# Pair preparation, scatters and shared expert taken out of the fixed order and emitted behind the scan

## The chip, the cores and the metric

The kernel runs on one core of one Trainium2 chip. The core has TensorE (PE, with its weight loads shown apart as PEld), VectorE (DVE), ScalarE (ACT), GpSimd (POOL) and SyncE (SP), each with a queue of its own that is worked off in order. The metric is the device time of one execution in microseconds; lower is better. Before the change the median of 13 runs is 1127.09 us (1125.89 to 1131.21).

## The reference

One layer of an adaptively modulated transformer block on `x` of shape (8, 512, 128), in float32:

```python
mod = (silu(c) @ wmod).reshape(8, 6, 1, -1)
sa, ca, ga, sb, cb, gb = ...           # the six parts; |ga|, |gb| at least 0.25
h = layernorm(x) * (1 + ca) + sa
x = x + ga * mamba(h)                  # 4 layers, then an RMS norm with final_norm_w
h = layernorm(x) * (1 + cb) + sb
x = x + gb * moe(h)
```

A layer of `mamba` norms `h`, projects it, runs a causal convolution of four taps with SiLU, a state-space scan over the 512 positions (8 heads of 32, state 128), a gated RMS norm and an output projection that is added to `h`. `moe` norms its input again, sends every token through a shared expert (128 to 512, ReLU, 512 to 128) and through the two experts of eight with the largest router probabilities, weighted by these, and adds the results:

```python
normed = h * rsqrt(mean(h * h) + 1e-8) * norm_weight
shared = relu(normed @ sw1 + sb1) @ sw2 + sb2
scores, idx = top_k(sigmoid(normed @ router_w.T), 2)
w = scores / (scores.sum(-1) + 1e-6)
routed = sum over the two: w * (relu(normed @ ew1[e] + eb1[e]) @ ew2[e] + eb2[e])
```

## The kernel before

**The scan.** A unit is one of the 8 sequences in one of the 4 layers (32 units), an item is a chunk of 128 positions of a unit (`NI` = 128 items). A loop over `t` emits the stages of several items, shifted against each other: the projections and the convolution of a unit run 16 steps (`LEAD * NC`) ahead of its items. From `p >= NI`, that is for the last 16 items, there is no next unit to project. For an item, `decay_rows` (L819) loads the cumulative decay row broadcast over the partitions, `decay_diff` (L838) subtracts on POOL, `decay_mask` masks on POOL, `decay_exp` (L859) takes the exponential on ACT, `mix` (L905) multiplies on DVE, `chunk_out` and `state_out` are products on TensorE, `state_decay` (L935, POOL) and `state_next` (L947) carry the state, `gate` (L984) and `project_out` (L994) follow, and `out_add` (L1018) adds the result to the residual `hs`, scaled by an inverse root that POOL takes (L1015). For the last 13 items `whole` (L834) is 4 instead of 8: POOL subtracts for four heads only, and ACT takes the other four as exponentials with the bias `ncum`, the negated sum that L809 writes.

**Pairs.** When two sequences have left the last layer, `rejoin` (L332) prepares them for the experts. It loads the modulation (`md`, L341), takes the final RMS norm (squares on ACT, `mean_squares` L320; inverse root by POOL for the first two pairs and by `power` L306 with small DVE instructions for the others; scaling on ACT, L356; product with `md` on DVE, L360), adds to `x`, takes the layer norm with its modulation, the second RMS norm, transposes the rows (L407), multiplies with the router weights (L415), chooses two experts for each token (L440 to L459), counts how many tokens of earlier columns and pairs go to each expert (`taken`, one table after the other), and puts 16 scatters per pair on a list: each writes 128 rows of the normed input with weight and token number to the list of their experts in DRAM, by `scatter` (L498) on POOL.

**Shared expert.** `shared` (L537) takes one sequence at a time: four products into four PSUM banks (L575), a ReLU out of each on ACT (L542), 16 products into one bank (L553) and a copy to `accs` (L546). It may run up to two evacuations late (`evacuate`). The hidden values take one of the five buffers that the scan's `xbc` has too.

**What sets the order.** The scan loop lies in `tc.manual_schedule()`: every engine issues its instructions in the order in which they are emitted. `rejoin`, `shared` and `tables` are generators, and the loop advances them at fixed places of a step: `rejoin` (`step_pairs`) once between `state_next` and `gate`, and once at the end of the step; `shared` (`serve`) once at the end of the step; one scatter per step ahead of `mix`. A pair begins two steps after its last item. What is left when the loop ends is woven by a second region of fixed order (from L1317), in which only POOL's order is left to the scheduler; it also holds `tables` (L1211, which expert each of the 39 tiles of 256 rows belongs to), `fetch` (L1256, loads of an expert's weights and, as `rest`, of its rows) and the loop over the tiles with `turn`, `hidden` and `combine`. Outside a fixed region the scheduler decides, from its own estimates of when operands are ready, where an instruction stands among the others of its engine; instructions emitted earlier have the higher priority.

**Buffers.** During the scan, pairs and the shared expert take PSUM banks from `pbank` (three banks). Behind it, pairs take them from three more (`psD`), and row buffers from a second pool (`frow2`, two buffers of each kind, as `frow`); `held` makes a pair wait where its row buffers are still to be scattered.

## Time and profile before

| | us |
|---|---|
| median of 13 runs | 1127.09 |
| profiled execution | 1127.32 |
| its span | 1124.9 |
| PE busy | 960.9 (85%) |
| DVE busy | 828.4 (74%) |
| ACT busy | 768.1 (68%) |
| POOL busy | 828.7 (74%) |
| last `out_add` of the scan ends | 840.6 |
| first scatter of the last pair starts | 909.5 |
| first `turn` on TensorE starts | 937.5 |

Times in the profile count from the start of the span. The busy shares are means over stages with different limits, so they don't tell what a change in one stage is worth. The profiled execution is one run; the 2.4 us between its span and its time lie around the span. A group "L862 ACT dV<-dV" is the instruction of line 862 on ACT that reads and writes the tile `dV`; the time after an arrow is how long the engine stood idle before, and what ended it. "remote" is a wait whose release the profile doesn't show. Float32 products show as two records each.

### The profile page before, as it was taken

To read this page: it belongs to the slowest core of one execution; us is meant where nothing else is said; L and a number is where in the kernel's file an instruction comes from. 1 tells how busy PE (TensorE), PEld (TensorE's weight loads), DVE (VectorE), ACT (ScalarE), POOL (GpSimd) and SP (SyncE) were. 2 spreads that over 40 slices of the span, in tenths; PEclk is the share of its full clock that TensorE was granted. 3 is DMA by queue.
4 is the path that set the end of the run, shared out by engine and by line. 5 is a ranking of instruction groups with operands and counts; after the bars stand their busy time and mean duration, and the time that the engine had idled before them with its cause. 6 is when DMAs were issued, how large, how long until landed. Compare 5 with 4: busy or idle time off the path is not lost. (4 is left out here: it accounts for less than half of the span.)

```text
span 1124.9 us, 21442 instructions
## 1 busy us (share of the span) xinstructions
PE 960.9 (85%) x7130; PEld 731.7 (65%) x7130; DVE 828.4 (74%) x1990; ACT 768.1 (68%) x1725; POOL 828.7 (74%) x841
## 2 busy tenths in 40 slices
PE   3667899999999999999999998687758756999985
PEld 1335677777777677777767776565545545888882
DVE  3758889889989889989889998586546163666653
ACT  4577998988988889889889878786336322333320
POOL 6868888989989989889989888685651552555550
PEclk9668999999999999999999999787867887999998
DMA  5141444655655555643424343422000125777756
GB/s 113 5 143 59 137 153 128 186 160 169 195 168 170 187 154 175 171 150 123 129 97 135 113 131 126 135 98 85 29 29 10 38 72 153 220 220 216 224 141 228
DMA packets 134301, 151.18 MB, mean 134 GB/s; under 512 B 22568, under 2 KB 106696, under 8 KB 134192
## 3 DMA queue, kind: packets, MB, share of 16 engines
q1 hardware_dynamic: 127184, 137.91, 41.4%
q0 software_dynamic: 4672, 9.42, 2.5%
q10 hardware_dynamic: 2336, 2.50, 0.7%
q8 instruction: 56, 0.92, 0.3%
q14 instruction: 53, 0.43, 0.1%
HBM read 120.07 MB, written 29.71 MB: 133 GB/s over the span
## 5 line engine op out<-in xcount | busy, mean ns | idle before, releaser
L698 DVE SCALAR_TENSOR_TENSOR xbc<-px,cw,xbc 128x511 f32<-128x511 f32 (+2 forms) x384 | 285.8, 745 | 31.4 <-ACT xbc L688 24.3
L841 POOL TENSOR_TENSOR dV<-dV,cum 128x1024 f32<-128x1024 f32 (+1 forms) x128 | 231.7, 1810 | 0.0
L907 DVE TENSOR_TENSOR dV<-dV,ptx 128x1024 f32<-128x1024 f32 x128 | 155.1, 1212 | 16.1 <-ACT xT L885 15.4
L849 POOL TENSOR_SCALAR_AFFINE_SELECT dV<-dV 128x1024 f32<-128x1024 f32 x128 | 141.7, 1107 | 9.3
L892 POOL TENSOR_TENSOR xd<-xT,dt 128x512 f32<-128x512 f32 (+1 forms) x128 | 120.5, 941 | 34.6 <-ACT xT L885 34.6
L500 POOL DMA_INDIRECT yg<-y,ix x78 | 84.1, 1078 | 83.9 <-DVE y L1313 69.4
L862 ACT ACTIVATE dV<-dV 128x1024 f32<-128x1024 f32 (+1 forms) x128 | 129.1, 1009 | 13.1 <-POOL dV L849 12.7
L500 POOL DMA_INDIRECT xg<-row,ix x64 | 63.4, 990 | 63.4 <-ACT hds L542 42.1
L688 ACT ACTIVATE xbc<-px,cbias,cw 128x512 f32<-128x512 f32 x128 | 99.3, 776 | 10.1 <-PE px L677 9.7
L677 PE MATMUL px<-hT,Wi 128*128 128x512 f32 x192 | 100.4, 605 | 0.0
L916 PEld LDWEIGHTS py<-xbc,st 128*128 128x128 f32 x384 | 61.3, 203 | 55.3 <-issue 38.0
L991 ACT ACTIVATE sq<-g 128x256 f32<-128x256 f32 x128 | 52.4, 410 | 58.3 <-DVE g L987 39.3
L1295 ACT ACTIVATE hd<-ph,bs 128x256 f32<-128x256 f32 x78 | 32.7, 470 | 83.4 <-PE ph L1289 74.4
L1007 PE MATMUL po<-Wo,g 128*128 128x128 f32 x512 | 89.4, 298 | 0.0
L1003 PEld LDWEIGHTS po<-ones,sq 128*128 128x128 f32 x512 | 68.3, 194 | 31.2 <-issue 21.3
L975 PE MATMUL py<-dV,xd 128*32 128x128 f32 x2048 | 85.4, 286 | 0.0
L965 PEld LDWEIGHTS py<-xbc,dg 128*128 128x128 f32 x512 | 79.0, 201 | 6.8 <-issue 1.0
L1003 PE MATMUL po<-ones,sq 128*128 128x1 f32 x512 | 78.7, 258 | 5.0 <-ACT sq L991 4.6
L965 PE MATMUL py<-xbc,dg 128*128 128x128 f32 x512 | 81.5, 284 | 0.0
L1302 PE MATMUL pe<-w,hd 128*128 128x128 f32 x624 | 75.9, 275 | 0.0
L1289 PE MATMUL ph<-xt,w 128*128 128x256 f32 x312 | 74.9, 384 | 0.1
L1302 PEld LDWEIGHTS pe<-w,hd 128*128 128x128 f32 x624 | 72.7, 192 | 0.1
(249 smaller groups left out, 2269.8 us busy)
## 6 DMA issues: line engine op xcount, KB each, us to landing
dV<-crow SPq DMA_DIRECT2D x128, 512.0 KB
w<-in_L_ffn_ew_dram SPq DMA_DIRECT2D x78, 256.0 KB
xg<-blank SPq DMA_DIRECT2D x64, 260.0 KB
ecum<-crow SPq DMA_DIRECT2D x256, 48.0 KB
rows<-xg SPq DMA_DIRECT2D x39, 130.0 KB
b<-in_L_ffn_eb_dram SPq DMA_DIRECT2D x39, 64.0 KB
x<-in_L_attn_x_dram SPq DMA_DIRECT2D x8, 256.0 KB
md<-mods SPq DMA_DIRECT2D x8, 256.0 KB
```

Of the source, the lines that this page charges most:

```text
L500: i = nc.gpsimd.indirect_dma_start(out=to, out_offset=bass.IndirectOffsetOnAxis(ap=ix, axis=0), in_=of, in_offset=None)
L677: nc.tensor.matmul(px[v, k][:, :L], Wi[l][:, c0 : c0 + P], hT[v], start=True, stop=True)
L688: nc.scalar.activation(xbc[v][:, k, :], px[v, k][:, :L], AF.Identity, bias=cbias[:, l, k : k + 1], scale=cw[:, l, k, KT - 1 : KT],)
L698: nc.vector.scalar_tensor_tensor(xbc[v][:, k, d:], px[v, k][:, : L - d], cw[:, l, k, KT - 1 - d : KT - d], xbc[v][:, k, d:], ALU.mult, ALU ...
L841: nc.gpsimd.tensor_tensor(dV[i][:, :w], dV[i][:, :w], cums[g][:, h0 : h0 + w].unsqueeze(2).to_broadcast([P, w, Q]), ALU.subtract,)
L849: nc.gpsimd.affine_select(out=dV[i], in_=dV[i], pattern=[[0, NH], [1, Q]], compare_op=ALU.is_ge, fill=-1e30, base=0, channel_multiplier=-1,)
L862: nc.scalar.activation(dV[i][:, :w], dV[i][:, :w], AF.Exp)
L892: nc.gpsimd.tensor_mul(xds[i][:, :w], xv.unsqueeze(1).to_broadcast([P, w, NH, HD]), dts[g][:, :w, h0 : h0 + NH].unsqueeze(3).to_broadcast( ...
L907: nc.vector.tensor_mul(Ms[i], Ms[i], pg.pop(i).unsqueeze(1).to_broadcast([P, NH, Q]))
L965: nc.tensor.matmul(py[i][:, k, :], dg[l][:, k, :], xbc[u][:, k, t], start=False, stop=True, skip_group_check=True,)
L1003: nc.tensor.matmul(pp[:, 2 * DM + c : 2 * DM + c + 1], sq[:, k, :], ones[:, 0:1], start=(k == 0), stop=(k == NB - 1))
L1302: nc.tensor.matmul(pe[:, s, :], hd[:, k, s * P : (s + 1) * P], w2[:, k, :], start=(k == 0), stop=(k == FK - 1))
```

## The change

The diff takes the pairs, their scatters and the shared expert out of the scan's loop and out of the woven part behind it. The fixed order of the scan is closed after the loop, and then, outside any fixed order, each pair is emitted whole, its scatters at once behind it; the shared expert of sequences 0 to 3 is emitted ahead of the last pair, that of sequences 4 to 7 behind it. `shared` becomes a plain function without late evacuations. All pairs now use `pbank`'s three banks and the first pool of row buffers. The split of the heads between POOL and ACT for the last 13 items is gone: POOL subtracts for all eight and ACT takes one exponential. In the first norm, the scaling on ACT and the product on DVE become one `scalar_tensor_tensor` on DVE per chunk. Behind the scan, the second fixed region starts with `tables`, and the first fetches come as experts 0 and 1 with their rows, then expert 2 with its rows.

```diff
@@ rejoin
         for j in range(n):
-            nc.scalar.activation(h[:, j, :], h[:, j, :], AF.Copy, scale=rs[:, j : j + 1])
-            if j % NC == NC - 1:
-                yield
-        for t, m in both(0):
-            nc.vector.tensor_mul(h[:, t, :], h[:, t, :], m)
+            nc.vector.scalar_tensor_tensor(
+                h[:, j, :], h[:, j, :], rs[:, j : j + 1], md[j // NC][:, 0, :], ALU.mult, ALU.mult
+            )
...
-        while scatters and scatters[0][0] in held.get(len(rowpools), [])[:-1]:
-            yield
-        held.setdefault(len(rowpools), []).append(g)
...
-        routed.update(seqs)
@@ shared
+    def shared(b):
+
+        hd = xbp.tile([P, NX, L], F32, tag="xbc", name=f"hds{b}")
+        for k in range(FK):
+            ph = pbank(f"phs{b}_{k}")
+            nc.tensor.matmul(ph[:, :L], w12[0][:, k * P : (k + 1) * P], hTx[b], start=True, stop=True)
             nc.scalar.activation(hd[:, k, :], ph[:, :L], AF.Relu, bias=b1[:, E, k : k + 1])
...
+        pe = pbank(f"pes{b}")
+        for s in range(NC):
             for k in range(FK):
+                nc.tensor.matmul(
+                    pe[:, s * DM : (s + 1) * DM],
+                    hd[:, k, s * P : (s + 1) * P],
+                    w12[1][:, k * P : (k + 1) * P],
+                    start=(k == 0),
+                    stop=(k == FK - 1),
+                )
+        accs[b] = hp[b // 2][:, b % 2]
+        nc.scalar.copy(accs[b].rearrange("p s d -> p (s d)"), pe)
@@ scan
-            if g >= (U - LEAD) // GROUP:
-                ncum[g] = scratch[:, m * (g % 2) : m * (g % 2 + 1)]
-                nc.vector.tensor_scalar_mul(ncum[g], cums[g], -1.0)
...
         def decay_diff(i):
             u, s, g, h0 = where(i)
-            w = whole(i)
             nc.gpsimd.tensor_tensor(
-                dV[i][:, :w],
-                dV[i][:, :w],
-                cums[g][:, h0 : h0 + w].unsqueeze(2).to_broadcast([P, w, Q]),
+                dV[i],
+                dV[i],
+                cums[g][:, h0 : h0 + NH].unsqueeze(2).to_broadcast([P, NH, Q]),
                 ALU.subtract,
             )
...
         def decay_exp(i):
-            u, s, g, h0 = where(i)
-            w = whole(i)
-            nc.scalar.activation(dV[i][:, :w], dV[i][:, :w], AF.Exp)
-            for h in range(w, NH):
-                nc.scalar.activation(dV[i][:, h, :], dV[i][:, h, :], AF.Exp, bias=ncum[g][:, h0 + h : h0 + h + 1])
+            nc.scalar.activation(dV[i], dV[i], AF.Exp)
...
-        actx.enter_context(tc.manual_schedule())
         gens = {}
+        fixed = actx.enter_context(ExitStack())
+        fixed.enter_context(tc.manual_schedule())
...
-            for g, seqs in enumerate(sets):
-                if t == NC * (U - B) + NC * (seqs[-1] + 1) + 2:
-                    gens["pairs", g] = rejoin(g)
...
-            if drain and scatters and item(t + 3):
-                scatter(*scatters.pop(0)[1:])
...
-            if drain:
-                step_pairs()
...
-            if drain and routed:
-                serve()
...
+        fixed.close()
+        for g, seqs in enumerate(sets):
+            if g == len(sets) - 1:
+                for b in range(B // 2):
+                    shared(b)
+            finish(rejoin(g))
+            while scatters:
+                scatter(*scatters.pop(0)[1:])
+        for b in range(B // 2, B):
+            shared(b)
@@ behind the scan
     with tc.manual_schedule(engines={*tc.nc.engines} - {mybir.EngineType.Pool}):
-        tail = list(gens.values())
-        fetched = []
-        table = None
-        while tail or serving or scatters or table or not tab:
...
-        for rest in fetched:
-            rest()
+        finish(tables())
+        for js in ((0, 1), (2,)):
+            for rest in [fetch(j) for j in js]:
+                rest()
         turn(0)
         turn(1)
         hidden(0)
```

More of the change, by code (lines that the diff above doesn't have):

```diff
@@ L298, in prepare_experts @@
         yield
-    hTx, scatters, rowpools, banks, held = {}, [], [frow], [], {}
+    hTx, scatters, rowpools, banks = {}, [], [frow], []
     sets = [(b, b + 1) for b in range(0, B, 2)]
-    routed = set()
-    scratch = scb.rearrange("p b q -> p (b q)")
     def power(v, name, on_pool):
@@ L1056, in stage @@
                 softplus_end(g - 1)
-        actx.enter_context(tc.manual_schedule())
         gens = {}
-        def step_pairs():
-            for key in list(gens):
-                if isinstance(key, tuple) and not step(gens[key]):
-                    del gens[key]
+        fixed = actx.enter_context(ExitStack())
+        fixed.enter_context(tc.manual_schedule())
         EARLY = 9
@@ L1317, in adaln_mamba_moe @@
     with tc.manual_schedule(engines={*tc.nc.engines} - {mybir.EngineType.Pool}):
-        tail = list(gens.values())
-        fetched = []
-        table = None
-        while tail or serving or scatters or table or not tab:
-            for g in list(tail):
-                if not step(g):
-                    tail.remove(g)
-            while scatters:
-                scatter(*scatters.pop(0)[1:])
-            serve()
-            for g in list(tail):
-                if not step(g):
-                    tail.remove(g)
-            serve()
-            if len(taken) == len(sets) + 1 and not tab:
-                table = tables()
-            if not step(table):
-                table = None
-            if not fetched and "to" in tab:
-                fetched = [fetch(j) for j in range(3)]
-            serve()
-        for rest in fetched:
-            rest()
+        finish(tables())
+        for js in ((0, 1), (2,)):
+            for rest in [fetch(j) for j in js]:
+                rest()
         turn(0)
```

55 lines of the change are left out of this document (1 added, 54 removed).

## The prediction

> **What bounds the kernel now.** I read first the busy shares of the page, then a table of stages, then the chain that ended last and the waits in the stage that the change touches, and last the queues of POOL and DVE in that stage. The table of stages (columns: start and end, length, busy time and instructions of PE, PEld, DVE, ACT, POOL, then TensorE clock, DMA share, GB/s) shows where the change can act:
>
> ```profile
> 634.00:701.00 67.00, 63.53 (x543) 47.35 (x543) 60.23 (x125) 57.67 (x118) 57.84 (x54) 1.00 0.37 123
> 701.00:841.00 140.00, 99.00 (x714) 77.49 (x713) 89.79 (x266) 84.68 (x273) 91.44 (x93) 0.77 0.25 78
> 841.00:910.00 69.00, 53.81 (x270) 38.31 (x271) 29.88 (x144) 37.09 (x97) 20.84 (x23) 0.82 0.07 22
> 910.00:938.00 28.00, 7.28 (x64) 7.05 (x63) 10.17 (x30) 1.28 (x3) 15.58 (x16) 0.69 0.42 116
> 938.00:1097.00 159.00, 149.57 (x1013) 135.41 (x1011) 93.02 (x297) 51.11 (x117) 83.14 (x77) 0.99 0.71 200
> ```
>
> Up to 701 us (item 112 of 128) TensorE is 95% busy: the scan is bound by it, and the change touches it only at its last items. From 938 us the experts run, TensorE 94% busy; the change leaves that loop alone. Between lie 237 us in which no engine is full: the end of the scan to the last `out_add` at 840.6, the last two pairs and most of the shared expert to 909.5, where the last scatters begin, and the scatters with the tables and first loads until TensorE starts at 937.5. All of the change falls in here.
>
> The chain that ended last names, behind the scan, TensorE with the shared expert and not the pairs:
>
> ```profile
> 840.05 0.61 DVE h L1023 x2
> ...
> 850.13 3.83 PE phs L575 x4
> 853.96 2.77 PE pes L553 x16
> ...
> 901.85 5.25 PE phs L575 x12
> ```
>
> The waits in 700 to 940 us (who waited for whom; us in total, times, longest) say that the last pair queues behind that work (`prob` waits 21.0 us once) and that queues also stand still for something the trace does not show ("remote"):
>
> ```profile
> ACT h L546 <- remote: 32.7, 2, 18.2
> DVE prob L440 <- ACT prob L437: 26.5, 2, 21.0
> DVE rg L1014 <- remote: 9.3, 1, 9.3
> ```
>
> The queues of POOL and DVE near 790 us matter most. Fifteen of the sixteen scatters of pair 0 are emitted behind the scan, where POOL's order is already the scheduler's, so this is a sample of how it places such work:
>
> ```profile
> 780.97 1.14 POOL L500 DMA_INDIRECT xg<-row,ix  x1 [1.24 <-DVE oh L489]
> ...
> 787.48 0.96 POOL L500 DMA_INDIRECT xg<-row,ix  x1 [0.30 <-issue]
> 788.46 0.74 POOL L1015 TENSOR_TENSOR rg<-rg,mhalf 128x2 f32<-128x2 f32 x1
> ...
> 801.54 0.96 POOL L500 DMA_INDIRECT xg<-row,ix  x1 [0.30 <-issue]
> 802.53 0.62 POOL L941 TENSOR_TENSOR st<-st,edec 128x256 f32<-128x256 f32 x1
> ```
> ```profile
> 789.24 0.61 DVE L1023 SCALAR_TENSOR_TENSOR h<-po,rg,h 128x128 f32<-128x128 f32 x2 [3.22 <-POOL rg L1015]
> 803.18 0.42 DVE L957 TENSOR_TENSOR st<-st,py 128x256 f32<-128x256 f32 x1 [4.64 <-POOL st L941]
> ```
>
> The scatters did not only fill holes: DVE waited 3.2 and 4.6 us for scan instructions that stood behind them. `mix` (L907) starts at 784.8, 795.5, 806.1 and 817.2, 10.8 us an item; at 736.3, 742.0, 746.8 and 751.8, with pair work but no scatters, it is 5.2.
>
> **The change part by part.** The sum is against the profiled execution, 1127.32 us (span 1124.9 and 2.4 around it), 0.2 us above the median of 1127.09.
>
> *Decay of the last 13 items.* Before, POOL subtracts for half the heads (L841, 1.05 us) and ACT does the rest in four exponentials with a bias; now POOL does all, 1.90 us by the rows of the earlier items. POOL gets 13 x 0.85 = 11 us more. ACT goes per item from 0.52 + 1.26 to 1.05 (pitch), 13 x 0.73 = 9.5 us less, and DVE loses two copies of 0.18; these are worth nothing, as ACT is busy 60% of this stage and waits for others. POOL's end is uncertain: 0 if its holes take it (91 of 140 us busy), 11 if the scan's end moves by all of it. I take 11: POOL's items would need 1.90 + 1.09 + 1.05 and the small ones, about 4.9 us of a 5.2 us item, so no hole is left for them beside scatters.
>
> *First norm.* A pair drops 8 ACT scalings (two groups of 1.28) and 2 DVE products (two of 0.64 at their pitch), and gets 8 `scalar_tensor_tensor` of 128x128; the nearest row is L1023, two in 0.60. So ACT -2.6, DVE +1.1 a pair. On the last pair's chain, 848.3 to 852.2 before, 3.9 us become 2.4: -1.5. Ends: -6 if all four pairs lie on the path, +4.4 if DVE is what the path waits for; DVE is 64% busy in this stage, so I stay at -1.5.
>
> Where DVE and POOL overlap, the trace shows longer instructions: `x` L362 takes 2.02 us beside a POOL `st` L941 of 1.58, against 1.22 and 0.61 elsewhere. The Trainium skill ("SBUF — State Buffer", the practical consequences on the shared port pair) states that a DVE instruction with two SBUF inputs and a POOL instruction that reads SBUF exclude each other for the whole instruction. The new instruction has two such inputs, and its 9.6 us against 5.1 us before would by that rule hold POOL 4.5 us longer: the sum below would end 4.5 higher. I leave it out, as only a few of these rows were lengthened.
>
> *First fetches.* SP fetches experts 0 and 1, then issues their rows, and only then fetches expert 2. A fetch without a stall is about 3.5 us (915.4 to 918.7), so rows 2 leave some 3 us later, near 938.7, and land in 3.5 us, at 942; TensorE needs them at 943.6, after the first two `hidden`. Cover 1.4 us, so nothing is paid; without it up to 3.5. The rows of 0 and 1 no longer stand behind fetch 2, which ended at 933.7 while the last scatter was issued by 930.2: -2 at best. I take -1.
>
> *What is moved.* Per pair: two `md` loads on SP (0.42 us each, moved behind the scan's row loads; needed only after the squares, so hidden by them, 0.9 a pair if not), on ACT 16 squares, 16 more scalings, two transposed copies and an exponential, on DVE the sums, tables and 3 x 11 small instructions of the inverse roots (POOL's three of 1.64 for pairs 0 and 1), on TensorE 8 transposes, 8 router products, 2 sums, and 16 scatters of 1.27 us on POOL. The shared expert is 32 products of 0.86 us and 128 of 0.22 us at their pitch (two records each), 7.0 us a sequence, and 40 ACT copies. No count changes. What changes is whom they stand in front of. Order of emission: pairs 0 to 2, shared 0 to 3, pair 3, shared 4 to 7.
>
> A pair alone, by the rows of the last ones: squares 3.5, root 2.5, first norm 2.4, sum and statistics 3.6, root and shift 2.6, scale, product and sum 5.2, squares 3.5, root 2.5, rows 2.6, transposes and copies 1.5, router and exponential 1.3, choice 4.6, sums and indices 4.6: 40 us with hand-offs. The last one took from 840.6 to 909.5, 69 us.
>
> Ends for the order: if the last pair runs alone (40) and the drain keeps 6.0 us an item (5.2 plus 0.85: 701 + 96 + 15 = 812), first turn comes at 812 + 40 + 20.3 for scatters + 7.3 for landing, rows and hand-off = 880, -58. If pair 2, shared 0 to 3 and pair 3 follow one another behind the scan (851, with the 11 us), it is 851 + 40 + 28 (TensorE's 4 x 7.0) + 40 + 27.6 = 987, +49. I choose by the nearest row, the scatters that the scheduler placed already. They cost the scan 11 us for 14 (two items of 10.7 instead of 5.2). Pair 1's sixteen come now at 823.9, behind nearly all POOL work of the scan; with the pairs free they can fall among its items as well: +12 to +15. In return the 9.3 us stop of DVE at 829 to 838, inside that burst, may go. Net +6. Of the rest I assume that the free order wastes as much as the order by hand.
>
> That 9.3 us stop and the 14.5 and 18.2 us of ACT, which end at 838.4, 896.5 and 932.8, lie in or just behind bursts of scatters, and from 873 to 898 the DMA answer has no packet on the instruction queues. The Trainium skill ("Runtime: NRT & Kernel Launch", Instruction fetch mechanics) says that refills are fetched ahead and mostly hidden; by that the bursts would cost only POOL's time and the sum would be 9 higher, there being no stop to win back. The measured stops speak against it, though no row proves what was fetched.
>
> Sum: 1127.3 + 11 - 1.5 - 1 + 6 = 1141.8, about 1142.
>
> **The rivals.** *The last pair runs free.* For it: with the fixed order the last pair waited 21 us for its router product behind shared products, and its own work is 40 of 69 us; free, with only shared 0 to 3 in front of it and 4 to 7 beside the scatters, where TensorE does 7 us of work in 28, it could lose 20 to 29 us. Even if the scan ends at 851, 851 + 40 + 27.6 = 919 against 937.5, -19; with the scan's end at 812, -58. I name 1096, -31, between them. Against it: the scatters above, which went in front of scan work. It decides as soon as the last pair's path shrinks by more than the 11 + 6 us that the scan's end loses.
>
> *The pairs pile up.* The free work gives way to the scan, pair 2 and shared 0 to 3 lie behind it, in front of pair 3, and all draw on three PSUM banks and two buffers of rows instead of the added ones behind the scan. By the upper end above it is up to +49; with part of pair 2 done, +30: 1157 to 1175. For it: shared 0 to 3 stand ahead of pair 3. Against it: ACT and DVE have 55 and 50 us free before 841.
>
> *It changes nothing.* The same work finds the same holes, and gains cancel losses: 1127. Little speaks for it, as the stage is sensitive to every order.
>
> **How the numbers follow.** A difference under 0.2% (2.3 us) can't be told from no change. Forecast, 1130 to 1155: 0.42. Last pair free, 1080 to 1124: 0.32. Pile-up, 1155 to 1185: 0.22. Nothing, 0.04. So slower 0.64, same 0.04, faster 0.32. As cases of both signs hold most of the chance, the forecast's own range is 1130 to 1155; the 8 in 10 range goes from 1088, which leaves out about a fifth of the gains, to 1175, which leaves out the worst third of the pile-up.
>
> **What would show it.** Right: POOL rows of L841 all at 1.90; scan items at 10 us or more wherever scatters stand in POOL's queue, and waits for `rg` or `st` behind them; last `out_add` near 855; last scatters beginning near 922; TensorE's first turn near 952; the expert loop still 159 us. Wrong: a first turn before 937, with the last pair under 58 us after the scan (the free pair), or shared products ahead of it that stretch it to 85 or more (pile-up). What would make the prediction wrong above all is how well the scheduler's estimates of readiness fit this stage, of which the trace of before shows one engine only.

## The result and the profile after

| | before | after |
|---|---|---|
| median, us | 1127.16 (40 runs) | 1176.0 (9 runs, 1170.5 to 1178.5) |
| profiled execution / its span | 1127.32 / 1124.9 | 1175.02 / 1173.2 |
| last `out_add` of the scan ends | 840.6 | 790.6 |
| first scatter of pairs 0, 1, 2, 3 | 781.0 (pair 0), 909.5 (pair 3) | 791.5, 836.6, 880.1, 932.9 |
| last scatter ends | 930.2 | 952.8 |
| first `turn` on TensorE | 937.5 | 983.2 |

The changed kernel is slower: the ratio is 1.0423, with a 95% interval of 1.0409 to 1.0438, which is 48.9 us. The forecast was 1142, and 1176.0 lies 1 us above the upper end of its range.

The table of stages of the kernel after, over the same kind of stretches as before (start and end, length, busy time and instructions of PE, PEld, DVE, ACT, POOL, then TensorE clock, DMA share, GB/s), is cut at the first scatter of each pair and at the first turn:

```profile
695.00:791.00 96.00, 79.65 (x714) 65.64 (x713) 77.04 (x181) 52.58 (x121) 76.21 (x68) 0.89 0.30 96
791.00:837.00 46.00, 7.46 (x28) 5.95 (x28) 13.95 (x80) 13.47 (x53) 19.20 (x19) 0.51 0.10 35
837.00:880.00 43.00, 10.66 (x33) 7.47 (x34) 20.80 (x105) 14.10 (x54) 15.80 (x16) 0.50 0.08 25
880.00:933.00 53.00, 40.75 (x191) 27.90 (x190) 16.32 (x83) 23.18 (x56) 16.35 (x17) 0.80 0.07 21
933.00:983.00 50.00, 28.96 (x157) 20.12 (x156) 10.37 (x31) 11.95 (x19) 15.22 (x16) 0.83 0.17 51
983.00:1143.00 160.00, 151.35 (x1014) 137.32 (x1014) 93.11 (x297) 51.12 (x117) 81.77 (x76) 0.98 0.74 203
```

The scan's end is 50 us earlier than before, and the stretch from there to the first turn is 95.7 us longer (192.6 for 96.9); with 2.6 us more from the first turn to the end this makes the 48.3 us of the spans' difference. In 791 to 880 us no engine is busy even half of the time: PE has 18 us of work in 89, DVE 35, ACT 28, POOL 35. The pairs come one after the other, 45, 43 and 53 us apart. So what was added is waiting and not work.

The waits of the kernel after, in 695 to 985 us (who waited for whom; us in total, times, longest), have these among the longest:

```profile
DVE full L1152 <- PE pn L1149: 34.5, 1, 34.5
...
ACT h L377 <- DVE off L374: 26.3, 1, 26.3
...
DVE off L374 <- POOL pyL L308: 22.5, 2, 19.7
...
ACT row L395 <- DMA xg<-row,ix: 10.9, 1, 10.9
...
ACT h L540 <- remote: 10.2, 2, 5.1
```

The timeline of the kernel after shows each of them in its queue (start, length, engine, instruction; in brackets the idle time of the engine and what ended it):

```profile
810.64 0.96 POOL L492 DMA_INDIRECT xg<-row,ix  x1 [0.31 <-issue]
811.62 1.68 POOL L308 TENSOR_TENSOR pyL<-pvL,mhalf 128x8 f32<-128x8 f32 x1
813.33 0.17 DVE L374 SCALAR_TENSOR_TENSOR off<-mvF,pyL 128x8 f32<-128x8 f32 x1 [19.69 <-POOL pyL L308]
813.53 0.88 ACT L377 ACTIVATE h<-x,off,pyL 128x128 f32<-128x128 f32 x2 [26.35 <-DVE off L374]
...
858.83 0.22 ACT L395 ACTIVATE row<-tok 128x8 f32<-128x8 f32 x1 [10.90 <-DMA xg<-row,ix]
...
875.45 0.66 PE L466 MATMUL pos<-mx,below 128*128 128x64 f32 x2 [4.37 <-DVE ptF L315]
875.90 2.02 PE L527 MATMUL phs<-h,ws 128*128 128x512 f32 x2
...
966.48 0.29 PE L1149 MATMUL pn<-taken,ones 128*128 128x8 f32 x2
966.80 0.29 DVE L1152 TENSOR_TENSOR full<-pn,ahead 128x128 f32<-128x128 f32 x1 [34.54 <-PE pn L1149]
```

Four things are to be seen. First, pair 1's root `pyL` on POOL stands behind the sixteen scatters of pair 0 (791.5 to 811.6), and DVE and ACT wait for it. Second, ACT stands before L395, which writes the row numbers of a later pair. It needs nothing of its pair but a row buffer; `frow` has two, and this one is free only when pair 1's scatters have landed. Pair 2's squares are queued behind it. Third, the shared expert of sequences 0 to 3 begins right behind pair 2's `pos`, though the input of sequences 0 and 1 was there near 760 and that of 2 and 3 near 825, and PE stood idle for most of the 85 us before; its 28 us of products then stand in front of pair 3. Fourth, `pn`, the tables' first product, stands behind all but the last 3.2 us of the shared expert of sequences 4 to 7.

The last wait in the list, "remote", has no release that the trace names. It was in the trace of before too and needs a word ahead of the experiments. The runs fell on five further chips, and the kernel before takes 1127 to 1131 us on two of them, as on the first, and 1110 us on three. In every trace from the first kind there are such stops beside the scatters; in none of the twelve from the second kind is there one in 700 to 990 us. I call them chips with and without stops, and compare only within a kind, by ratios to the kernel before on the same chip. Each chip was used for one batch of runs only, so what belongs to the chip and what to the batch can't be told apart.

### The profile page after: what moved, and what is told of

The parts are those of the page before. It is cut to its first block, busy times and chain, and to the rows that moved or that the text cites. A ratio compares the mean times of both kernels' runs of the same rounds, so it can differ in the third digit from the quotient of the medians.

```text
span 1173.2 us, 21431 instructions
## 1 busy us (share of the span) xinstructions
PE 964.0 (82%) x7130; PEld 734.0 (63%) x7130; DVE 831.0 (71%) x2012; ACT 751.2 (64%) x1641; POOL 838.6 (71%) x841
## 5 line engine op out<-in xcount | busy, mean ns | idle before, releaser
L783 POOL TENSOR_TENSOR dV<-dV,cum 128x1024 f32<-128x1024 f32 x128 | 244.2, 1908 | 2.4 <-DMA dV<-crow 2.4
L802 ACT ACTIVATE dV<-dV 128x1024 f32<-128x1024 f32 x128 | 134.8, 1053 | 20.1 <-POOL dV L791 19.8
```

The lines of the kernel that those rows point to most:

```text
L783: nc.gpsimd.tensor_tensor(dV[i], dV[i], cums[g][:, h0 : h0 + NH].unsqueeze(2).to_broadcast([P, NH, Q]), ALU.subtract,)
L802: nc.scalar.activation(dV[i], dV[i], AF.Exp)
```

## The experiments

Theory Q: in queues that run in order, freely placed instructions that wait for something stand in front of instructions that could run. Its rivals are theory S (stops and slower instructions beside the scatters set the time) and theory C (the cost of the changed operations themselves: heads and norm). Ratios to the kernel before, with 95% intervals:

| kernel | chip without stops | chip with stops |
|---|---|---|
| after | 1.0355 [1.0337, 1.0372] | 1.0423 [1.0409, 1.0438] |
| `dve_root` | 1.0375 [1.0351, 1.0400] | |
| `pn_first` | 1.0227 [1.0208, 1.0246] | |
| `shared_by_pair` | 1.0209 [1.0181, 1.0237] | |
| `late_col` | 1.0274 [1.0255, 1.0294] | |
| `root_late` | | 1.0225 [1.0204, 1.0247] |
| `all_four` (twice) | 0.9967 [0.9947, 0.9986], 0.9975 [0.9956, 0.9994] | |
| `heads_back` | 1.0305 [1.0273, 1.0337] | |
| `norm_only` | 1.0080 [1.0061, 1.0098] | |
| `order_only` (twice) | | 1.0375 [1.0350, 1.0401], 1.0334 [1.0300, 1.0367] |
| `best` | | 1.0169 [1.0139, 1.0200] |
| `before_again` | | 1.0004 [0.9984, 1.0023] |
| `four_dve` (twice) | 0.9965 [0.9951, 0.9980] | 1.0051 [1.0023, 1.0079] |
| `best_dve` | 0.9954 [0.9940, 0.9968] | |
| `before_dve` | 1.0008 [0.9997, 1.0019] | |

A difference in the third digit is turned into us with 1110 on the first kind and 1127 on the second; differences of two ratios are uncertain by some 3 us.

**The changed kernel on a chip without stops.**

> The changed kernel, unchanged, on the chip that runs its variants: what they are to be measured against. In its first profile ACT stood idle 5.0 us before 891.7 and 4.9 before 902.4 with nothing named to wait for or on a late PE product, and the same instructions took 885.4 to 909.6 there and 885.1 to 897.7 in the variant with pn emitted first. Theory S (stops of the supply belong to this program, or come and go): the ratio to the kernel before is 1.042 again if they belong to the program, and 1.030 to 1.036 if they do not recur, since they are 12 us. Theory Q alone expects 1.040 to 1.044.

1.0355: the stops did not recur. In the kernel after on the first chip ACT's copy of the first shared result waits for no named cause, and the same instruction on the other chip does not (timeline of the kernel after, then of its repetition):

```profile
885.39 1.26 ACT L377 ACTIVATE h<-x,off,pyL 128x128 f32<-128x128 f32 x3 [0.91 <-DVE pyL L316]
891.70 0.58 ACT L540 COPY h<-pes 128x512 f32<-128x512 f32 x1 [5.04 <-remote]
```
```profile
885.01 1.26 ACT L377 ACTIVATE h<-x,off,pyL 128x128 f32<-128x128 f32 x3 [0.37 <-DVE off L374]
886.85 0.59 ACT L540 COPY h<-pes 128x512 f32<-128x512 f32 x1 [0.58 <-PE pes L532]
```

Up to 880 us the two traces agree within 0.5 us, with the last `out_add` at 790.6 and 790.1. Pair 3's first scatter is at 932.9 and 919.5, the first turn at 983.2 and 959.7. So of the 48.9 us, 39.4 (0.0355 x 1110) are there without any stop; the other 9.5 go with the chip.

**The roots on DVE.** In `rejoin`:

```diff
-        on_pool = g < 2
+        on_pool = False
```

> The changed kernel with one word changed: the roots of all four pairs are made on DVE (as pairs 2 and 3 already have them) and none on POOL. Theory Q (a freely placed instruction holds up the in-order queue that it was put in): in the kernel after, pair 1's root pyL starts at 811.62, right behind the 16 scatters of pair 0 on POOL, and DVE's L374 and ACT's L377 wait 19.7 and 26.4 us for it; with the root on DVE pair 1 comes some 15 to 20 us earlier (its first scatter 16.. before 836.6), and the time falls by 12 to 20 us, to 1156 to 1164. Theory S (stops of the instruction supply and the shared port set the tail): the wait for POOL goes and the time is what it was within 4 us, as each root on DVE is 12 small instructions more. Theory C (the operations' own cost, the POOL heads and the fused norm): no change within 3 us.

The ratio did not fall (1.0375 against 1.0355). The timeline of this kernel shows why:

```profile
803.61 0.17 DVE L374 SCALAR_TENSOR_TENSOR off<-mvF,pyL 128x8 f32<-128x8 f32 x1
803.81 3.19 ACT L377 ACTIVATE h<-x,off,pyL 128x128 f32<-128x128 f32 x8 [12.13 <-DVE off L374]
...
818.37 0.22 ACT L395 ACTIVATE row<-tok 128x8 f32<-128x8 f32 x1 [10.97 <-DMA xg<-row,ix]
```

`off` does come 9.3 us earlier (803.6 for 812.9 in `after_again`), but at 818.4 ACT has waited 11.0 us before a later pair's row numbers until pair 0's scatters landed. The second wait took the place of the first: pair 1's scatters begin 42.9 us behind pair 0's, for 45.2. These 2.3 us are more than lost at another place, as the scan ends 5.0 us later in this kernel (795.1 for 790.1). Theory Q had said 12 to 20 us less and was wrong; theories S and C had said no change, and their numbers came true, but the reason is a second wait in a queue.

**The row numbers behind the pair's weights.** On DVE, with a product that ties them to the pair:

```diff
-        for c in range(2):
-            nc.scalar.activation(rows[c][:, :, DM + 1], tok[:, :n], AF.Copy, bias=float(c * T + b0 * L))
...
             nc.vector.tensor_mul(rows[c][:, :, DM], w, den)
+            col = t2(f"col{c}")
+            nc.vector.tensor_scalar(col, w, 0.0, float(c * T + b0 * L), ALU.mult, ALU.add)
+            nc.vector.tensor_add(rows[c][:, :, DM + 1], col, tok[:, :n])
```

> The changed kernel with the row-number column (L395, on ACT, needing nothing of its pair but the row buffer) made on DVE behind the pair's own weights, four small DVE instructions in place of two on ACT. Theory Q: in the kernel after, ACT stands from 847.9 to 858.8 before pair 3's L395, which waits for the scatters of pair 1 to land and free the row buffer, with pair 2's squares queued behind; without it pair 2 and with it all later work come 8 to 11 us earlier, 1165 to 1168. Theory S or C: no change within 3 us, or 1 us longer for the instructions added.

9.0 us less than `after_again` (1.0274), as Q said: pair 2's first scatter is 32.8 us behind pair 1's for 43.6 before, and the 10.8 us gained reach the first turn as 9.8 (949.9 for 959.7).

**Both, to see the two waits in series.**

> The changed kernel with two edits, all roots on DVE and the row-number column on DVE behind the weights. Alone, the roots gave +0.002 (nothing) and the column -0.008 of the time before. In the kernel with the roots alone, pair 1's off came 9.3 us earlier (803.6 for 812.9), but then ACT waited 11.0 us before L395 for pair 0's scatters to land, so the second wait took the place of the first. Theory Q with the two waits in series: together they give more than the sum, pair 1's first scatter 10 to 13 us earlier than in the changed kernel, and a ratio of 1.0355 - 0.016 to 0.024 = 1.012 to 1.020. If the root costs nothing in any order: 1.027 to 1.030.

This run fell on a chip with stops, so it is read against 1.0423: 22.3 us less, while the single edits add up to 6.8 (9.0 less and 2.2 more, on the other kind). Pair 1's first scatter moved from 836.6 to 825.6, pair 2's from 880.1 to 860.6. Counted from the last `out_add`, pair 1's first scatter comes at 35.7 us, for 46.1 in `after_again`, 43.8 with the roots alone and 46.1 with the row numbers alone: the root gains little as long as the other wait stands behind it. Not all of the surplus is this. The later end of the scan that the roots alone cost isn't here (789.9 for 795.1), which no run explains, and the single edits were measured on the other kind of chip.

**The tables' product first.**

```diff
+        pn = pbank("pn")
+        nc.tensor.matmul(pn[:, :E], ones, taken[-1], start=True, stop=True)
         for b in range(B // 2, B):
             shared(b)
...
-        pn = banks[-1]("pn")
-        nc.tensor.matmul(pn[:, :E], ones, taken[-1], start=True, stop=True)
```

> The changed kernel with the first product of the tile tables (pn) emitted ahead of the shared expert of sequences 4 to 7 rather than behind it. Theory Q: in the kernel after, DVE's L1152 waits 34.5 us for pn, which stands on PE behind that shared expert though its operand was ready near 932; with pn ahead the tables are ready before the last scatter is issued at 952.8, and the first turn moves from 983.2 to 958 to 968, the time to 1150 to 1162. Theory S or C: the first turn is held by the fetches behind the scatters or by the shared expert's work itself, which PE has to do before or among the loop; the time falls by less than 5 us.

14.2 us less (1.0227); the first turn is at 943.9 for 959.7, with `pn` at 915.8 for 942.6. That is the low end of what Q said, since the wait for `pn` is 24.1 us and not 34.5 without the stops (`after_again`), and since the rows of the first tiles can't be read before the last scatters (938.7) have landed.

**The shared expert by pairs.**

```diff
         for g, seqs in enumerate(sets):
-            if g == len(sets) - 1:
-                for b in range(B // 2):
-                    shared(b)
             finish(rejoin(g))
             while scatters:
                 scatter(*scatters.pop(0)[1:])
-        for b in range(B // 2, B):
-            shared(b)
+            for b in seqs:
+                shared(b)
```

> The changed kernel with the shared expert of each pair's two sequences emitted right behind that pair's scatters, in place of sequences 0 to 3 ahead of pair 3 and 4 to 7 behind it. Theory Q (PSUM banks and queues go by the order of emission): the shared expert then starts in the stretch 760 to 837 in which PE is busy 7.5 of 46 us, none of the 28 us of it stands between pair 2 and pair 3 or behind the last scatters but for sequences 6 and 7; the last pair's first scatter moves from 932.9 by 0 to -15 us, the first turn by -10 to -30, the time is 1146 to 1166. Theory S or C: PE's order is not what holds the pairs, the pairs stay 43 to 53 us apart, and the time changes by less than 5 us.

16.2 us less (1.0209). The shared expert starts at 790.8, right behind pair 0's `pos` (790.6), as in the kernel after it starts right behind pair 2's: its place follows the place of its emission among the pairs, and not the time at which its input is ready. Whether the hand-out of the PSUM banks or the scheduler's ranking does it was not tried. The gain came otherwise than I said: pair 1 was 6.3 us later (842.5 for 836.2) and pair 3 no earlier than 918.6 for 919.5, as products and evacuations now stand between all pairs; what moved the first turn, 946.2 for 959.7, is `pn` at 928.7 for 942.6 with only two sequences in front of it.

**The four together**, with `pn` right behind the last pair's scatters and ahead of that pair's shared expert.

> The changed kernel with four edits at once: all roots on DVE, each pair's shared expert behind its own scatters, the tables' first product right behind the last pair's scatters and ahead of that pair's shared expert, the row-number column on DVE behind the pair's weights. Theory Q: the edits take away different waits (20 us of POOL, 11 us of ACT, 14 us of PE behind pair 2, 18 us of PE ahead of the tables), so their gains add up for the larger part: 40 to 65 us below the changed kernel, a ratio to the kernel before of 0.985 to 1.005. Theory S: the gains of the single edits were mostly the absence of the stops, 12 us in each of them, and do not add up: a ratio of 1.010 to 1.025.

0.9967: 43.1 us less than `after_again`, somewhat more than the 37.2 that the single edits add up to, and all of the 39.4 that the change costs on this kind of chip. The stages of this kernel, cut at the first scatters and the last:

```profile
796.00:830.00 34.00, 21.89 (x106) 16.20 (x105) 22.21 (x113) 18.44 (x60) 16.08 (x17) 0.75 0.16 48
830.00:863.00 33.00, 23.64 (x109) 17.01 (x108) 19.49 (x109) 19.51 (x62) 16.40 (x17) 0.75 0.10 33
863.00:895.00 32.00, 22.52 (x109) 16.71 (x108) 17.24 (x92) 15.36 (x44) 15.52 (x17) 0.77 0.10 34
895.00:919.00 24.00, 14.98 (x79) 10.29 (x79) 9.36 (x25) 6.67 (x10) 15.84 (x16) 0.86 0.37 106
```

The pairs' first scatters are 33, 33 and 32 us apart, for 45, 44 and 40 in `after_again` on the same chip, each stretch with two sequences of the shared expert in it, and the first turn comes 24 us behind the last of them (918.9) for 40. Against S, the gains of the edits do add up.

**The parts that are no order.** The heads split again between POOL and ACT as in the kernel before:

```diff
         def decay_diff(i):
             u, s, g, h0 = where(i)
+            w = whole(i)
             nc.gpsimd.tensor_tensor(
-                dV[i],
+                dV[i][:, :w],
...
         def decay_exp(i):
-            nc.scalar.activation(dV[i], dV[i], AF.Exp)
+            nc.scalar.activation(dV[i][:, :w], dV[i][:, :w], AF.Exp)
+            for h in range(w, NH):
+                nc.scalar.activation(dV[i][:, h, :], dV[i][:, h, :], AF.Exp, bias=ncum[g][:, h0 + h : h0 + h + 1])
```

> The changed kernel with the last 13 items' heads split between POOL and ACT again as in the kernel before (POOL does half of each subtraction, ACT the other half as a bias). The prediction priced the undoing of this split at 13 x 0.85 = 11 us on POOL's stream, and the scan of the changed kernel runs at 5 to 5.5 us an item there with POOL's subtraction at 1.90. If POOL's stream bounds those items, the scan's end and with it the pairs come 8 to 11 us earlier: a ratio 0.008 to 0.010 below the changed kernel's. If ACT, which has the pairs' squares and 4 more exponentials for each item, becomes the bound, or the tail is set by waits between the pairs, it changes by less than 3 us or is slower by up to 5.

5.5 us less (1.0305 for 1.0355). The scan's last `out_add` is 8.3 us earlier (781.8 for 790.1), pair 0's first scatter only 3.5 (787.5 for 791.0), and the first turn 3.8: by then the pair's own chain, and not the scan, seems to end last.

The norm alone, in the kernel before:

```diff
         for j in range(n):
-            nc.scalar.activation(h[:, j, :], h[:, j, :], AF.Copy, scale=rs[:, j : j + 1])
-            if j % NC == NC - 1:
-                yield
-        for t, m in both(0):
-            nc.vector.tensor_mul(h[:, t, :], h[:, t, :], m)
+            nc.vector.scalar_tensor_tensor(
+                h[:, j, :], h[:, j, :], rs[:, j : j + 1], md[j // NC][:, 0, :], ALU.mult, ALU.mult
+            )
```

> The kernel before with one part of the change alone: the first norm's scale made by DVE in one instruction with the product of the modulation (8 scalar_tensor_tensor for 8 ACT copies and 2 DVE products in each pair), the order by hand kept. The prediction priced it at -1.5 us with ends of -6 and +4.4. Theory C (cost of the operations, with the shared port stretching an instruction of 0.34 us to 1.1 beside POOL): +1 to +5 us. Theories Q and S: within 2 us of the kernel before.

1.0080, 8.9 us more, outside what any theory said. The groups of the kernel with the norm alone (line, engine, names, shape, count; busy us, mean ns), and behind them those of the kernel before:

```profile
L356 DVE SCALAR_TENSOR_TENSOR h<-h,pyF,md 128x128 f32<-128x128 f32 x32 | 17.1, 602 | 1.4 <-POOL pyF L310 1.4
L360 DVE TENSOR_TENSOR x<-x,h 128x1024 f32<-128x1024 f32 x4 | 8.0, 2005 | 0.0
```
```profile
L356 ACT ACTIVATE h<-h,pyF 128x128 f32<-128x128 f32 x32 | 10.2, 393 | 2.1 <-DVE ptF L317 2.1
L360 DVE TENSOR_TENSOR h<-h,md 128x512 f32<-128x512 f32 x8 | 6.6, 859 | 2.3 <-ACT h L356 2.3
L362 DVE TENSOR_TENSOR x<-x,h 128x1024 f32<-128x1024 f32 x4 | 5.7, 1417 | 0.0
```

DVE has 25.1 us of work for 12.3. The new instruction takes 0.34 us in the median of its 32 and up to 1.98, and the sum behind it grows too. The last POOL subtraction of the scan begins at 806.0 for 796.3 in `before_dve` (the kernel before with one copy moved, which comes below), and the last `out_add` ends at 853.8 for 840.7. The first part of this is lost at pair 0, whose eight instructions stand in one block in front of an item's `mix` (the kernel with the norm alone, then `before_dve`):

```profile
689.86 6.34 DVE L356 SCALAR_TENSOR_TENSOR h<-h,pyF,md 128x128 f32<-128x128 f32 x8
...
697.04 1.21 DVE L905 TENSOR_TENSOR dV<-dV,ptx 128x1024 f32<-128x1024 f32 x1
```
```profile
691.11 1.21 DVE L907 TENSOR_TENSOR dV<-dV,ptx 128x1024 f32<-128x1024 f32 x1
```

The edit also takes out two places (`yield`) at which a pair gives way to the scan, so the length of the eight and their standing in one block are not separated. The execution in the profile is the fastest of this kernel (1115.4 for a median of 1118.4), and its first turn is only 3.2 us later (927.4 for 924.2): how the whole of the 8.9 us comes about is not shown.

The order alone, with heads and norm as before:

> The changed kernel with two parts of the change undone, so that of the change only the order (the free emission behind the scan and the fetches) is left: the last 13 items' heads are split between POOL and ACT, and the first norm's scale is made by ACT with DVE's product, as in the kernel before. The prediction had the order at +5 us (+6, and -1 for the fetches), the heads at +11 and the norm at -1.5. The runs on this chip so far have the whole change at 1.0355, the heads at 0.005 of it and the norm, in the order by hand, at 0.008. If the parts add up, the order alone is 1.0355 - 0.005 - 0.008 = 1.020 to 1.026; if the fused norm costs nothing where the pairs run behind the scan (DVE is idle there), 1.029 to 1.033; by the prediction's terms 1.002 to 1.008.

Both runs fell on chips with stops (1.0375 and, repeated, 1.0334), where the whole change is 1.0423: the order alone costs 38 to 42 us there, heads and norm together 5 to 10. These include the stops, which differ: before the copy of the shared result ACT stands 20.2 and 15.0 us in the two traces of this kernel, and 10.2 in the kernel after. On a chip without stops the order alone was not run.

> The order alone (heads and norm undone) once more. On a chip where the kernel before shows 1110 us, the whole change is 1.0355 and the heads are 0.005 of it: 1.022 to 1.026 if the fused norm costs 0.008 here too, 1.029 to 1.033 if it costs nothing behind the scan. On a chip where it shows 1127 us: 1.035 to 1.040 again.

**The attempt to beat both kernels, and the stops.**

> The four edits together (0.9967 of the time before) and, beside them, the heads split again and the norm's scale back on ACT, so that of the change only the free order is left and its four waits are mended. If the single gains add up (0.004 for the heads, 0.000 to 0.008 for the norm): 0.984 to 0.993, faster than both kernels. If the pairs' own chain of 32 to 33 us each now bounds everything between the scan's end and the first turn, and the heads only bring the scan's end forward: 0.990 to 0.995.

It did not: 1.0169, 19 us above the kernel before. Its list of waits has one long entry that none of the edits aimed at:

```profile
ACT h L542 <- remote: 42.7, 4, 14.7
```

The chip is one with stops, and this order runs the shared expert beside every burst of scatters. The kernel before, on the same chip:

> The kernel before, unchanged, on this chip, for its trace: its profile on the other chip has three stops of 9.3, 14.5 and 18.2 us in which DVE and ACT wait for nothing that the trace names. Theory S (they belong to the chip or the launch, not to the order): none of them is in this trace, the first turn comes 14 to 18 us earlier than 937.5, and the ratio is 1.000. If they belong to the program they stand at the same instructions again.

The stops came again at the same two copies, 14.55 and 18.14 us for 14.46 and 18.23 on the first chip, and DVE's with 8.6 for 9.3. So they belong to the chip and to the place in the program together; that they are an accident of one launch is refuted.

To see what they hang on, the copy of the shared expert's second product was given to DVE:

```diff
-        nc.scalar.copy(accs[b].rearrange("p s d -> p (s d)"), pe)
+        nc.vector.tensor_copy(accs[b].rearrange("p s d -> p (s d)"), pe)
```

> The four edits together once more, for comparison on one chip with the kernels beside it. If the stops before ACT's copy come with the chip: on a chip where the kernel before shows 1127 us it has 25 to 45 us of them, as it runs the shared expert beside the scatters, and a ratio of 1.000 to 1.020; on a chip where the kernel before shows 1110 us, 0.995 to 0.999 again. If the stops belong to the program of the kernel called best alone: 0.995 to 0.999 on any chip.

> The four edits, and the copy of the shared expert's result from PSUM made by DVE in place of ACT (8 copies of 128x512, about 0.6 us each). If the stops hang on ACT's copy waiting in ACT's queue: they are gone, and it is 20 to 40 us faster than the four edits alone on a chip with stops. If they hang on PE's product being reported late, DVE stands there instead, and with it the pairs' own DVE work: within 5 us of the four edits, or slower. On a chip without stops: within 3 us of the four edits.

> The kernel before with that one copy on DVE in place of ACT. Its trace on the second chip has ACT waiting 14.5 and 18.1 us before two of these copies. If the stops hang on ACT's copy: 10 to 25 us faster on such a chip, and the first turn near 915 to 925 for 937. If the product is reported late whoever asks for it: within 4 us. On a chip without stops: within 3 us.

These three fell on a chip without stops and could only show that the copy's engine is worth nothing there: 0.9975, 0.9965 and 1.0008.

> The four edits with the shared expert's copy on DVE, once more. On a chip where the kernel before shows 1127 us: 0.985 to 1.000 if the stops hang on ACT's copy, 1.005 to 1.020 if they come whoever copies. On a chip where it shows 1110 us: 0.995 to 0.998 again.

1.0051, on a chip with stops. The timeline of this kernel there:

```profile
840.77 3.06 PE L533 MATMUL pes<-ws,hds 128*128 128x128 f32 x26
...
843.67 1.88 PE L528 MATMUL phs<-h,ws 128*128 128x512 f32 x4
...
847.59 0.69 DVE L541 COPY h<-pes 128x512 f32<-128x512 f32 x1 [4.74 <-remote]
847.63 0.69 ACT L529 ACTIVATE hds<-phs,b 128x512 f32<-128x512 f32 x1 [2.71 <-remote]
```

The stops moved with the copy, 36.4 us on DVE and 15.1 on ACT. DVE and ACT wait for two different products of PE and go on within 0.04 us of each other. So it is not ACT and not its copy that stands: what both wait for is that PE's products count as done, some 4 us after the trace's modelled end of the first. The trace's semaphore events say so as well: each of these five stops ends within 0.1 us of an update of a semaphore that only PE's instructions raise. Three of the five stops on DVE end 2.1 to 2.5 us behind the last issue of a burst of scatters (815.5, the burst's last issue ending at 813.0, for one), two inside a burst.

**What is left of heads and norm in the mended order.**

> The same with the heads split again and the first norm's scale back on ACT. Against the kernel with the four edits and DVE's copy on the same chip it shows these two parts without the stops: 4 to 12 us faster if the single prices add up (heads 0.004, norm 0.000 to 0.008 of the time before), slower by 5 to 15 if the norm back on ACT costs the pairs behind the scan more than the fused form, as ACT is then in front of DVE in each pair's chain.

0.9954 against 0.9965 for `four_dve` on the same chip, with overlapping intervals: undoing heads and norm together is worth 1 us or nothing there; the two were not separated in this order. It is the fastest kernel of the study on a chip without stops, 0.5% faster than the kernel before; on a chip with stops the nearest kernel that was run, `four_dve`, is 0.5% slower. So no version here was shown to beat the kernel before on both kinds.

## Why the prediction was wrong

*Where the time is lost* was right in the main: the expert loop kept its length (190.0 us from first turn to the end, for 187.4), and nearly everything happened between the scan's last items and the first turn. The exception is pair 0's first norm, at 690 us, in the stretch that the prediction left out.

*Heads, +11.* POOL's rows are at 1.90 (median of L783 in 695 to 791 us, with single ones up to 2.88), and the scan's end moved 8.3 us for them. The time moved by 5.5 in the changed kernel; in the mended order heads and norm together show 1 us or nothing. The term was twice too large: of the scan's 8.3 us only 3.5 reach pair 0's first scatter.

*First norm, -1.5, ends -6 and +4.4.* Wrong in sign in the order by hand: +8.9 us. What failed in it is the price of 0.30 us from L1023, taken for all 32; they take 0.60 in the mean. DVE gained 12.8 us for the 4.4 that I had as the upper end. And I took DVE as 64% busy, as it is from 701 us on; pair 0's eight stand at 690 us, where the table of stages has DVE busy for 60.23 of 67 us, and the next `mix` is 5.9 us later for them. The rule that I left out was the nearer one: the Trainium skill ("SBUF — State Buffer", the consequences on the shared port pair) excludes a DVE instruction with two SBUF inputs and a POOL instruction that reads SBUF from each other. The rows agree in that an instruction of 0.34 us took up to 1.98; its sum of +4.5 put the wait on POOL's side, whereas here POOL's subtractions kept their length (1.06 us in the mean for half the heads, 1.055 in `before_dve`) and DVE's instructions grew. In the mended order it was not priced by itself.

*First fetches, -1.* Not tried by itself.

*Order, +6.* This is the step that failed and made the forecast wrong, by some 35 us. The order alone measured +38 to +42 on the same kind of chip, its stops included; on a chip without stops the whole change costs 39.4, and without the heads' 5.5 some 34 are left for the order, the fetches and the norm together. It failed at two places. First, the sample: from fourteen scatters that stood among the scan's items I inferred that pair 1's would stand there too. In the kernel after none does: all 64 are behind the scan, no item takes 10 us, and the scan ends at 790.6, not near 855. The sample's price was misread too, as items of 9.9 and 10.3 us (`mix` from 720.8 to 730.6 and from 758.5 to 768.9) stand in the trace of before ahead of the first scatter at 781.0. The whole change ends the scan 50 us earlier than before, where I had it later. Second, the assumption "of the rest I assume that the free order wastes as much as the order by hand". It wastes more: from the end of the scan to the first turn the whole change takes 95.7 us longer, for which the sum had nothing. The four edits show where: a root behind scatters on POOL, row numbers on ACT that wait for a buffer, the shared expert behind the third pair on PE, the tables' product behind the shared expert. Together they gave back 42 to 43 us where the change costs 39.

*The 9.3 us stop of DVE* that I had going did go with the scatters in the scan. ACT still has two in the kernel after, of 5 us each. That the supply of instructions causes them is not shown: in `best` a packet of the instruction queues falls into the stop that ends at 849.6 (at 842.5 to 843.0), and none into that which ends at 901.2. The Trainium skill ("Runtime: NRT & Kernel Launch", Instruction fetch mechanics) calls refills mostly hidden. No run here decides whether the stops have to do with refills.

*The rivals.* The pile-up had 0.22 and a price of up to +49; the measured 48.9 is its upper end, and its sign (85 us or more from the scan to the last pair) came as 142. But the sum agreed by luck. It had the scan's end at 851, and that was 790.6; it had one pair, the shared expert and the last pair behind it, and there were three whole pairs at 45, 43 and 53 us. Two of its reasons, two buffers of rows and shared 0 to 3 ahead of pair 3, are among the four waits shown; the three PSUM banks were not tested. The free last pair (0.32) never came about: it was fourth in line.

## What to carry to other kernels

Work that is emitted outside a fixed order is not thereby out of the way: on each in-order queue it stands in front of something, so before freeing work list, engine by engine, the instructions that need only a buffer (they are placed early and then wait for it), those that share a queue with a burst of DMA issues, and those that start the next stage. When a mended wait brings nothing, look for the next wait in the same stretch before calling it harmless: here a root worth nothing by itself was followed by a second wait, and both together brought pair 1 forward by more than the single edits add up to. Measure the kernel before on the same chip each time: the same two programs differed by 3.6% on one chip and by 4.2% on another.

## What the runs showed of the hardware

On some chips the same program is slower than on others, by 17 to 21 us (kernel before) and up to 29 us (`four_dve`, 1134.9 and 1105.5), with waits of 3 to 18 us in which the readers of TensorE's products stand beside POOL's indirect scatters. A clock that is lower throughout doesn't explain this: the kernel after keeps its times within 0.5 us up to 880 us on both kinds. The waits go with the product and not with the engine that reads it, and are in none of twelve traces of the other kind. ACT's two in the kernel before recur within 0.1 us on two chips (14.46 and 14.55; 18.23 and 18.14), but those of `order_only` do not (15.0 and 5.1, then 8.5 and 6.5). Of the 21 such waits of over 4.5 us before the copy of the shared expert's result, in eight traces, 13 end 1.1 to 3.1 us behind the end of a burst's last issue, which is 2.0 to 4.0 us behind its start, and 8 inside a burst. On a chip without stops the median scatter whose landing is known lands 2.3 us behind the start of its issue (`after_again`). All 21 end within 0.1 us of an update of TensorE's own semaphore, and 15 have no packet of the instruction queues inside them.

In the stop of 14.46 us TensorE's own records stand apart. Some 16 of them start between 884.3 and 896.4, in groups of one to three, with idle time between that ends with nothing but their issue; in `before_dve`, on a chip without stops, the same products follow each other in 0.11 us:

```profile
885.77 0.51 PE L553 MATMUL pes<-ws,hds 128*128 128x128 f32 x3 [1.14 <-issue]
...
890.72 0.81 PE L553 MATMUL pes<-ws,hds 128*128 128x128 f32 x3 [2.23 <-issue]
...
896.45 0.58 ACT L546 COPY h<-pes 128x512 f32<-128x512 f32 x1 [14.46 <-remote]
```

So there TensorE itself seems to go on haltingly, and the profile of the same kernel on the second chip shows the same. In the stop that ends at 932.8 the records are close together and the last starts at 916.5. What holds the products stays open: TensorE's ends are modelled in the trace, and a kernel without scatters was not run.
